# Layer 3 of a four-layer kernel: order of the sums on TensorE, and which engine multiplies states 3 and 12 by C

## The chip, the cores and the metric

The kernel runs on one core of a Trainium2 chip. The metric is device time in microseconds for one launch, the median of several runs. Engines: TensorE (PE, with its weight loads PEld), VectorE (DVE), ScalarE (ACT), GpSimd (POOL), and SyncE (SP), which here only issues DMAs.

## The reference

Four layers run one after another on an image batch of 8 x 64 channels x 64 x 64 in f32. The change touches layer 3 alone. That layer is a pair of bidirectional state-space scans (Mamba), first along t and then along f. Cut to what matters:

```python
xc = silu(causal_dwconv(xc, cw, cb))
dbl = xc @ xpw.T                       # dt (rank r), B and C (n = 16 states each)
dt = softplus(dbl[..., :r] @ dtw.T + dtb)
def step(h, inp):                      # for every channel d and state n
    dA = exp(dt_t[:, :, None] * A)
    h = h * dA + (dt_t * x_t)[:, :, None] * B_t[:, None, :]
    y = einsum('bdn,bn->bd', h, C_t)
```

So each of the 16 states needs: dA = exp(dt*A), the product du*B (du = dt*x), the recurrence h, the product h*C, and the sum of h*C over the states.

## The kernel before, in words

**Tiles.** In layer 3 one *step* handles 512 positions of 256 channels, laid out as a tile of 128 partitions x 1024 (two halves of channels side by side). There are 256 steps: 2 weight sets x 16 chunks x 4 groups x 2 directions (the list `steps` at the end of `layer3`). Each step runs over 16 states, so the loop `for i in range(total + 2)` in `stream` has 4096 iterations; `n` is the state, `i % 16`.

**Work for one state.** ScalarE makes dA (`decay`, L522), two iterations ahead or three. The product du*B comes from one of two places. For states 0, 3, 4, 7, 8, 11 to 15 GpSimd multiplies (`multiply_b`, L528), three iterations ahead. For states 1, 2, 5, 6, 9, 10 (`fed`, called `direct` in `stream`) TensorE makes it with eight 128x128 matmuls against a diagonal matrix (`expand`, L2257): into a PSUM tile of the `dA` ring for 1, 5, 9 (`lent`), into the single PSUM tile `mm` for 2, 6, 10. Both of a pair are issued in one iteration: 5 and 6 in iteration 3, 9 and 10 in iteration 7, 1 and 2 of the next step in iteration 15. VectorE scans (`scan`, L552). The product with C (`multiply_c`, L566) is GpSimd's for the states listed in `shared` and VectorE's for the others. TensorE then adds the product into the PSUM tile `acc` with four 64x512 identity matmuls (`gather` calling `quads`, L320); this is called the state's *sum* below. Groups named `acc<-h` are sums of GpSimd's states, those named `acc<-hc` of VectorE's.

**Buffers.** A state of GpSimd's is scanned into a tile `h` of a pool of three, is multiplied by C there in place, and holds the tile until its sum has been read. A state of VectorE's is scanned in place in its `dA` tile (a ring of two PSUM tiles), and its product goes to a tile `hc` (three). The products du*B and the exponents of the `fed` states share a pool `hb` of four, used in the order of the states. Rows of B and C, broadcast to 128 partitions, come by DMA into a pool `bc` of eight, fetched six states ahead (`fetch`, L2266 to L2270); a slot comes free when the C product of its state is done.

**What sets the order.** Nothing is reordered: every engine runs its instructions in the order in which the loop writes them. In an iteration that is: fetch, `multiply_b(i+3)`, GpSimd's `multiply_c(i-1)`, pieces of the next step's preparation (`plan` says how many and where), sums, other tasks (`advance`), `scan(i)`, further pieces, VectorE's `multiply_c(i)`, `decay` and `expand`. The pieces that matter here are the matmul to B, C and dt (L2195, written behind scan 2), the matmul for dt (L2207, iteration 3, before the scan), du on GpSimd (L2217, iteration 4), the gate's matmul (L2224, behind scan 6), the transposes of du (L2246, behind scan 10) and the convolution's matmul (L2180, behind scan 13). All of these use the single PSUM tile `mm`. State 0's sum is written behind scan 2 (`first`), with the skip term (`acc<-u,skip`) before it.

## Time and profile before

| what | value |
|---|---|
| median of 3 runs | 23591.48 us (23584.76 to 23625.18) |
| the profiled execution's own time | 23561.4 us |
| its span, first to last instruction | 23559.6 us |
| layer 3's scans, in the span | 11202 to 23551 us |
| VectorE busy in that stretch | 11846.8 of 12349.0 us |
| GpSimd busy in that stretch | 11478.2 us |
| TensorE busy (matmul / weight load) | 10683.0 / 5648.0 us |
| ScalarE busy | 9143.4 us |
| granted TensorE clock, DMA share | 0.95, 0.63 |

Costs of the operations that recur, mean of one:

| operation | engine, line | ns |
|---|---|---|
| product du*B | GpSimd, L528 | 2366 |
| product h*C | GpSimd, L566 | 2361 |
| product h*C | VectorE, L566 | 1225 |
| scan | VectorE, L552 | 2269 to 2282 |
| exponents, two of 512 columns | ScalarE, L522 | 689 to 711 each |

How to read it: a group's row in the profile names the line, engine, operation, what it writes and reads, and a count, then its busy time, the mean of one, and how long its engine was idle just before, with what ended most of that. Helpers hide the state number: all scans are L552 and all sums are L320, so a single state is found by its place in the timeline of a step. Between two scans the C product of VectorE makes the distance 3.45 us instead of 2.19. A step of 16 states takes 48.23 us on average, and the shortest about 46.5.

### The profile page before, as it was taken

To read this page: it belongs to the slowest core of one execution; us is meant where nothing else is said; L and a number is where in the kernel's file an instruction comes from. 1 tells how busy PE (TensorE), PEld (TensorE's weight loads), DVE (VectorE), ACT (ScalarE), POOL (GpSimd) and SP (SyncE) were. 2 spreads that over 40 slices of the span, in tenths; PEclk is the share of its full clock that TensorE was granted. 3 is DMA by queue.
4 is the path that set the end of the run, shared out by engine and by line. 5 is a ranking of instruction groups with operands and counts; after the bars stand their busy time and mean duration, and the time that the engine had idled before them with its cause. 6 is when DMAs were issued, how large, how long until landed. Compare 5 with 4: busy or idle time off the path is not lost. (4 is left out here: it accounts for less than half of the span.)

```text
span 23559.6 us, 306615 instructions
## 1 busy us (share of the span) xinstructions
PE 19078.5 (81%) x108058; PEld 8425.2 (36%) x108058; DVE 21365.9 (91%) x12265; ACT 14942.1 (63%) x19503; POOL 20571.2 (87%) x9876
## 2 busy tenths in 40 slices
PE   7757776777777788878888888888888888888888
PEld 5311221221221223322444444444444444444444
DVE  5599999999999769977999999999999999999999
ACT  5445555555555456632777777777777777777776
POOL 0499999999999749975999999999999999999999
PEclk9878888888888899989999999999999999999999
DMA  3599999899999759951666666666666666666665
GB/s 80 193 328 331 316 317 330 313 320 325 315 322 321 261 174 340 343 184 39 181 186 183 184 182 184 185 182 182 183 183 186 182 184 182 184 183 183 184 184 173
DMA packets 2857413, 5296.53 MB, mean 225 GB/s; under 512 B 1357208, under 2 KB 1363452, under 8 KB 2853568
## 3 DMA queue, kind: packets, MB, share of 16 engines
q1 hardware_dynamic: 2831296, 5213.58, 69.6%
q10 hardware_dynamic: 24576, 63.33, 0.7%
q8 instruction: 854, 13.99, 0.2%
q14 instruction: 687, 5.63, 0.1%
HBM read 5112.98 MB, written 162.40 MB: 224 GB/s over the span
## 5 line engine op out<-in xcount | busy, mean ns | idle before, releaser
L528 POOL TENSOR_TENSOR hb<-du,bc 128x1024 f32<-128x1024 f32 x3072 | 7222.4, 2364 | 619.2 <-DMA bc<-bc 253.6
L552 DVE TENSOR_TENSOR_SCAN dA<-dA,hb 128x1024 f32<-128x1024 f32 x2488 | 5675.5, 2281 | 187.3 <-POOL hb L528 113.4
L566 POOL TENSOR_TENSOR h<-h,bc 128x1024 f32<-128x1024 f32 x2208 | 5180.4, 2361 | 118.2 <-DVE h L552 109.9
L528 POOL TENSOR_TENSOR hb<-du,b 128x1024 f32<-128x1024 f32 x2048 | 4879.7, 2417 | 336.2 <-DVE h L552 121.2
L522 ACT ACTIVATE dA<-dt,w_A 128x512 f32<-128x512 f32 x5120 | 3520.3, 689 | 1508.2 <-DVE hc L566 716.3
L522 ACT ACTIVATE dA<-dt,w_l_A 128x1024 f32<-128x1024 f32 x2560 | 2857.6, 1117 | 997.6 <-DVE hc L566 756.7
L552 DVE TENSOR_TENSOR_SCAN dA<-dA,carry,hb 128x1024 f32<-128x1024 f32 x1320 | 3093.8, 2344 | 95.1 <-POOL hb L528 52.9
L566 DVE TENSOR_TENSOR hc<-dA,bc 128x1024 f32<-128x1024 f32 x2400 | 2939.1, 1225 | 141.4 <-issue 2.7
L320 PE MATMUL acc<-h,ident 64*64 64x512 f32 x16384 | 2165.9, 629 | 399.6 <-POOL h L566 397.4
L2257 PE MATMUL dA<-bc,duT 128*128 128x128 f32 x12288 | 1854.5, 313 | 616.0 <-ACT z L2233 596.1
L2257 PEld LDWEIGHTS dA<-bc,duT 128*128 128x128 f32 x12288 | 1700.7, 222 | 1225.0 <-ACT z L2233 800.8
L320 PE MATMUL acc<-hc,ident 64*64 64x512 f32 x16384 | 2085.5, 602 | 0.0
L522 ACT ACTIVATE hb<-dt,w_A 128x512 f32<-128x512 f32 x3072 | 2039.3, 711 | 10.7
L1290 PE MATMUL acc<-hc,ident 64*64 64x512 f32 x11264 | 1857.0, 756 | 142.6 <-DVE img L1410 84.1
L552 DVE TENSOR_TENSOR_SCAN h<-hb,mm 128x1024 f32<-128x1024 f32 x768 | 1742.4, 2269 | 236.0 <-PE acc L320 168.1
L1290 PE MATMUL acc<-h,ident 64*64 64x512 f32 x5120 | 976.6, 834 | 1130.8 <-POOL h L566 1122.0
L552 DVE TENSOR_TENSOR_SCAN h<-hb,dA 128x1024 f32<-128x1024 f32 x768 | 1752.6, 2282 | 129.0 <-PE dA L2257 83.7
L566 DVE TENSOR_TENSOR hc<-dA,c 128x1024 f32<-128x1024 f32 x1408 | 1723.7, 1224 | 116.0 <-DMA c<-bc 3.8
L552 DVE TENSOR_TENSOR_SCAN h<-dA,hb 128x1024 f32<-128x1024 f32 x712 | 1622.9, 2279 | 17.6 <-ACT dA L522 16.8
L2257 PE MATMUL mm<-bc,duT 128*128 128x128 f32 x12288 | 1571.3, 283 | 1.4 <-ACT u L2191 1.4
L566 POOL TENSOR_TENSOR h<-h,c 128x1024 f32<-128x1024 f32 x640 | 1520.9, 2376 | 19.5 <-ACT carry L1383 19.0
L2257 PEld LDWEIGHTS mm<-bc,duT 128*128 128x128 f32 x12288 | 1521.8, 202 | 2.2 <-ACT u L2191 2.2
(344 smaller groups left out, 26991.6 us busy)
## 6 DMA issues: line engine op xcount, KB each, us to landing
bc<-bc SPq DMA_DIRECT2D x2560, 512.0 KB
b<-bc SPq DMA_DIRECT2D x2048, 512.0 KB
c<-bc SPq DMA_DIRECT2D x2048, 512.0 KB
bc<-bc SPq DMA_DIRECT2D x512, 1024.0 KB
bc<-dg SPq DMA_DIRECT2D x1536, 256.0 KB
bc<-bc SPq DMA_DIRECT2D x1536, 256.0 KB
tmp<-rs SPq DMA_DIRECT2D x93, 512.0 KB
raw<-x SPq DMA_DIRECT2D x256, 128.0 KB
```

The source lines that it names most:

```text
L320: self.nc.tensor.matmul(acc[j * C : j * C + C, r * 512 : r * 512 + 512], lhsT(j)[at, at], rhs[at, j * 512 : j * 512 + 512], start=start, s ...
L522: nc.scalar.activation(o[:, cut], s.dt[:, cut], AF.Exp, scale=A[:, n : n + 1])
L528: nc.gpsimd.tensor_tensor(s.shaped(hb[i]), s.shaped(s.du), B.pop(i), ALU.mult)
L552: nc.vector.tensor_tensor_scan(h[:, way], dA[i][:, way], b[:, way], s.first(n), ALU.mult, ALU.add)
L566: engine.tensor_tensor(s.shaped(o), s.shaped(h), CC.pop(i), ALU.mult)
L1290: nc.tensor.matmul(o, lhsT[at, at], part, start=start, stop=stop)
L2257: nc.tensor.matmul(hb[:, at], self.duT[:, at], diag[:, m * 128 : m * 128 + 128], start=True, stop=True)
```

## The change

It does two things, both in layer 3. In iteration `i` the sum of state `i-2`, where that is one of GpSimd's, is now written behind VectorE's C product and ahead of `decay` and `expand`; it was written in the next iteration (as `gather(i - 3)`) before the scan. And the list `shared` loses 12 and gains 3.

```diff
                 work = None if work and work.over else work
-                if 2 < i <= total + 2 and shared(i - 3):
-                    gather(i - 3)
                 if 1 < i and not first and not shared(i - 2):
                     gather(i - 2)
...
                 if i < total and not shared(i):
                     multiply_c(i)
+                if 1 < i and shared(i - 2):
+                    gather(i - 2)
                 if not direct(i + 2):
                     decay(i + 2)
...
-                    self.shared = (1, 2, 5, 6, 9, 10, 12, 14)
+                    self.shared = (1, 2, 3, 5, 6, 9, 10, 14)
```

Built, the two kernels have the same instructions in the same numbers. ScalarE's and SyncE's order is the same. On TensorE the sums of states 1 and 5 now stand in front of the expansions of 5, 6 and of 9, 10, and those of 2 and 6 right behind them; state 12's sum, still in front of the expansions of 1 and 2, is no longer one that waits for GpSimd. On GpSimd, state 3's C product stands between the du*B product of state 7 and `du`, and state 12's is gone from between the du*B product of the next state 0 and the C product of 14. On VectorE scans 1 to 4 follow without state 3's C product between them, and state 12's stands between scans 12 and 13.

## The prediction

> **What bounds the kernel now.** I read the page first, then VectorE's waits inside layer 3, then the timeline of one step of layer 3. Busy tenths in 40 slices (page):

> ```profile
> DVE  5599999999999769977999999999999999999999
> POOL 0499999999999749975999999999999999999999
> PEclk9878888888888899989999999999999999999999
> ```

> Layer 3 is the second half: its scans run from 11202 to 23551 us, 256 steps of 16 states, 48.23 us a step. VectorE and GpSimd are both over 90% busy there. The part on the chain that ended last shows 0% everywhere (it breaks off near the end), so it is of no use, and I take VectorE's waits in that stretch (columns: total us, times, longest):

> ```profile
> DVE h L552 <- PE acc L320: 168.1, 213, 1.8
> DVE h L552 <- PE dA L2257: 83.7, 182, 1.9
> DVE h L552 <- ACT hb L522: 73.1, 49, 4.5
> DVE dA L552 <- POOL hb L528: 28.2, 5, 26.0
> DVE h L552 <- ACT dA L522: 27.0, 34, 0.8
> ```

> VectorE loses little: a step without any wait takes 46.49 us (the one that starts at 17040.5), so 1.74 us of 48.23 is waiting. All that this edit could ever win in layer 3 is 256 x 1.74 = 445 us (1.9%). "PE acc" is a scan that wants one of the three `h` buffers back, which the additions on TensorE (L320) still read. Now TensorE and VectorE in the step whose scan 2 ends at 17145.54 (start, us, engine, line, operation; idle before in brackets):

> ```profile
> 17145.60 1.93 PE L2195 MATMUL mm<-u,w_xp 128*68 128x512 f32 x4 [0.96 <-DVE h L552]
> 17147.46 1.09 PE L320 MATMUL acc<-u,skip 64*64 64x512 f32 x8
> 17148.37 1.04 PE L320 MATMUL acc<-hc,ident 64*64 64x512 f32 x8
> 17149.34 1.13 PE L2207 MATMUL mm<-dbl,both 4*128 4x512 f32 x4
> 17150.40 2.05 PE L2257 MATMUL dA<-bc,duT 128*128 128x128 f32 x16
> 17152.28 1.95 PE L2257 MATMUL mm<-bc,duT 128*128 128x128 f32 x16
> 17154.16 1.95 PE L320 MATMUL acc<-h,ident 64*64 64x512 f32 x16
> ...
> 17161.51 3.65 PE L2257 MATMUL dA<-bc,duT 128*128 128x128 f32 x16 [2.35 <-ACT z L2233]
> 17164.95 1.99 PE L2257 MATMUL mm<-bc,duT 128*128 128x128 f32 x16
> ```
> ```profile
> 17148.90 1.23 DVE L566 TENSOR_TENSOR hc<-dA,bc 128x1024 f32<-128x1024 f32 x1
> 17150.04 2.29 DVE L552 TENSOR_TENSOR_SCAN dA<-dA,hb 128x1024 f32<-128x1024 f32 x1
> 17152.36 1.22 DVE L566 TENSOR_TENSOR hc<-dA,bc 128x1024 f32<-128x1024 f32 x1
> 17153.50 2.28 DVE L552 TENSOR_TENSOR_SCAN h<-hb,dA 128x1024 f32<-128x1024 f32 x1
> 17155.69 2.26 DVE L552 TENSOR_TENSOR_SCAN h<-hb,mm 128x1024 f32<-128x1024 f32 x1
> ...
> 17165.26 2.29 DVE L552 TENSOR_TENSOR_SCAN h<-hb,dA 128x1024 f32<-128x1024 f32 x1 [0.34 <-PE dA L2257]
> ```

> To be seen: from scan 2's end TensorE works without a gap up to the du*B products of states 5 and 6 (17150.40 and 17152.28). State 5's product ends at 17152.45, only 1.05 us before scan 5 (17153.50), and what keeps scan 5 until then is state 3's and 4's C products on VectorE. Later TensorE idles 2.35 us, and state 9's product then takes 3.65 instead of 2.05.

> **The change, part by part.** Durations are of the one profiled execution (span 23559.6, time 23561.4 us; the median of the runs, 23591.48, lies 0.13% above). Means are over the 248 inner steps, from the timeline's rows. The frame is scan 2's end = 0.

> *State 3 to GpSimd, 12 to VectorE.* Counts stay: 8 products on each engine, 2361 ns on GpSimd (L566 POOL row), 1225 on VectorE. Scan 12 now runs in place like the others of VectorE's states (2281 against 2279 ns). On VectorE a C product between two scans adds 3.45 - 2.19 = 1.26-1.28 us, so state 3's leaves (-1.28), state 12's comes (+1.26): nothing by itself, but the scans 5 to 12 now want their inputs 1.28 us earlier.

> *Sum of state 1 ahead of state 5's product.* State 1's product on GpSimd ends at 0.32 (mean), so no wait is added, but TensorE reaches that point only at 4.9-5.1 in every step, and the sum takes its 0.91 us (start to start in the rows above) there. Expansion 5 ends now at 7.17 (mean; 6.91 in most steps), then at 7.17 + 0.91 = 8.08; a scan follows 0.10 later: 8.18. VectorE alone would be ready at 7.96 - 1.28 = 6.68. **New wait at scan 5: 1.50 us** (now 0.10). Queued behind on TensorE: expansion 6.

> *Scan 6's buffer.* The order of `h` buffers is now 1, 2, 3, 5, 6, ..., three deep, so scan 6 takes state 2's, and the sum of state 2 stands right behind expansion 6. Expansion 6 ends now at 8.96, then 9.87. Where a scan already waits for a sum behind an expansion, it starts 1.18 us after the expansion's end (0.91 plus release; state 10 in the median step): 11.05. VectorE: 8.18 + 2.19 = 10.37. **New wait 0.68** (now 0.12).

> *Scans 9 and 10.* Now they lose 0.94 us together: expansion 9 cannot start before state 7's C product frees its buffer (3.55 after scan 6's end), runs slow, and sum 5 stands behind expansion 10. After: GpSimd's order is product 7 (start 3.4, as scan 3 frees its buffer), **C 3**, du, B 8, C 5, five times 2.34: C 5 ends at 15.15, which is 2.1 after scan 6's new end (13.06-13.3; now 0.9 after). du waited 0.6 us for ScalarE before; that is absorbed. Sum 5 then ends 3.0 after scan 6's end, 0.5 ahead of the moment when expansion 9 may start. If TensorE stays warm, scans 9 and 10 go without a wait, as today in the steps where something else fills that gap (scan 10 at 9.08 after scan 6's end instead of 10.17). [...] I take 0.31: 0.1 each for the steps with an `xn` product in GpSimd's way (one in eight), for those where state 7's rows land late (44 of 248), and for a slow clock. Bounds 0.05 and 0.7.

> *Scans 1 and 2.* Now they lose 0.57: sum 12 waits for GpSimd's product 12 (0.3 after scan 15's end) and holds expansion 1. State 12 being VectorE's, that goes; expansion 1 then starts behind L2180 and sums 12 and 13, about 0.6-0.9 earlier. What is left is ScalarE's (the ACT hb row, in two steps of eight): 0.33. Bounds 0.2 and 0.57.

> *Other queues.* SP: state 11's rows go into state 3's buffer, now freed by GpSimd at 8.1 (16.7 after scan 0) and not by VectorE; SP issues them today at 17.0 on average, so nothing moves; if its slack were gone, B 11 has 2 us more. The next step's state 4 rows no longer wait for GpSimd's product 12 (issued 6 us earlier). GpSimd's B 8 ends at 12.8, scan 8 starts near 18.8; B 15 at 34, scan 15 at 37: covered. ScalarE's exponents keep their order and over 2 us.

> *Sum a step:* 1.50 + 0.68 + 0.31 + 0.33 = 2.82 of waiting against 1.74, so +1.08 us, x 256 = **+276 us** (1.2%): 23561.4 becomes 23837, the median 23591.5 becomes 23867. With the bounds, +0.68 to +1.75 a step: 23765 to 24040.

> **The rivals.**
> *Free additions, release early (faster).* The additions are small; if the array took sums 1 and 2 in the shadow of the du*B matmuls' weight loads, scan 5 would wait only 7.27 - 6.68 = 0.59 and scan 6 not at all: 0.59 + 0.31 + 0.33 - 1.74 = -0.51 a step, -130 us, 23461. It decides at 0.5 us: above it a sum ahead of expansion 5 eats what state 10 gains. Against: TensorE's rows are 0.91-0.97 from start to start around every such sum. 8%.
> *Free additions, release late (no change).* Scan 6 still 1.18 behind expansion 6: 0.59 + 0.68 + 0.31 + 0.33 - 1.74 = +0.17, +44 us, 23636: the wait has only moved from state 10 to 5 and 6. 9%.
> *GpSimd late and TensorE cold (slower still).* TensorE now stands waiting for C 5 with expansions 9 and 10 behind it. Spare is 0.5 us; if C 5 comes 0.5 later or the clock halves in three steps of four as now, sum 5 takes 1.9 and expansion 9 up to 3.65: 0.7 to 1.3 us more a step, 24050 to 24200. For it: GpSimd idles only 3.4 us a step. Against: the gap before it is shorter than today's. 17%.
> *As summed:* 66%.

> **How the numbers follow.** The prediction is the likeliest case, 23867. The range 23630 to 24120 takes in that case, the no-change case and the near half of the last; about 2 in 10 is left out. Faster or slower counts from 0.2% (47 us), about what a measurement of this kernel can tell: faster 0.08, same 0.09, slower 0.83.

> **What would show it.** VectorE's waits in layer 3: "h <- PE dA" grows from 84 to some 350 us, all at scan 5; "h <- PE acc" stays near 170 but sits at scan 6, not 10; state 9's expansions take near 2.05 on average; ACT hb stays near 70. Step length 49.3. I am wrong if scan 5 starts less than 7.5 us after scan 2's end (the sum costs nothing), or if waits for GpSimd's C 5 open in front of expansion 9.

## The result, and the profile after

The changed kernel takes 23929.75 us (median of 4 runs, 23922.62 to 23936.63) against 23594.22 us before (4 runs on the same chip): ratio 1.0142, 95% interval 1.0129 to 1.0155. That is 335.5 us, or 1.31 us for each of the 256 steps. The prediction was 23867 us, in the range 23630 to 24120.

The profiled execution took 23936.63 us with a span of 23934.8 us. The same three rows of the page as before:

```profile
DVE  5599999999999679977999999999999999999999
POOL 0499999999999669976999999989999999899998
PEclk9878887887888899999999999999999999999999
```

The rows hardly differ from those of before: a loss of 1.4% is invisible in tenths. The list of VectorE's waits in layer 3 (total us, times, longest) shows it:

```profile
DVE h L552 <- PE dA L2257: 402.3, 167, 3.6
DVE h L552 <- POOL h L566: 165.6, 127, 1.7
DVE h L552 <- PE acc L320: 137.7, 252, 0.6
...
DVE h L552 <- ACT hb L522: 14.6, 8, 4.0
```

"PE dA" grew from 83.7 to 402.3 us, and a wait for "POOL h" of 165.6 us appeared that did not exist. Where they sit is seen in the timelines of two neighbouring steps. First TensorE, then VectorE, in the step whose scan 2 ends at 16785.01 (the profile records each of these f32 matmuls twice, so x8 are the four of a sum):

```profile
16785.07 1.93 PE L2195 MATMUL mm<-u,w_xp 128*68 128x512 f32 x4 [1.26 <-DVE h L552]
16786.93 1.09 PE L320 MATMUL acc<-u,skip 64*64 64x512 f32 x8
...
16789.87 1.09 PE L320 MATMUL acc<-h,ident 64*64 64x512 f32 x8
16790.89 2.05 PE L2257 MATMUL dA<-bc,duT 128*128 128x128 f32 x16
16792.78 1.95 PE L2257 MATMUL mm<-bc,duT 128*128 128x128 f32 x16
```
```profile
16790.55 1.22 DVE L566 TENSOR_TENSOR hc<-dA,bc 128x1024 f32<-128x1024 f32 x1
16793.07 2.29 DVE L552 TENSOR_TENSOR_SCAN h<-hb,dA 128x1024 f32<-128x1024 f32 x1 [1.30 <-POOL h L566]
16795.91 2.29 DVE L552 TENSOR_TENSOR_SCAN h<-hb,mm 128x1024 f32<-128x1024 f32 x1 [0.55 <-PE acc L320]
```

The sum of state 1 (16789.87) now stands in front of expansion 5, which ends at 16792.94. Scan 5 follows 0.13 us later and has waited 1.30 us. The profile names GpSimd as its releaser only because GpSimd's product of state 3 happens to end at that moment (it started at 16790.71); scan 5 reads nothing of it. Then scan 6 waits 0.55 us for the sum of state 2.

The step before it (scan 2's end at 16734.83):

```profile
16734.88 2.74 PE L2195 MATMUL mm<-u,w_xp 128*68 128x512 f32 x4 [2.16 <-DVE h L552]
16737.55 1.93 PE L320 MATMUL acc<-u,skip 64*64 64x512 f32 x8
...
16741.32 1.09 PE L320 MATMUL acc<-h,ident 64*64 64x512 f32 x8
```
```profile
16744.53 2.29 DVE L552 TENSOR_TENSOR_SCAN h<-hb,dA 128x1024 f32<-128x1024 f32 x1 [2.94 <-PE dA L2257]
```

The order is the same, but TensorE had idled 2.16 us instead of 1.26, its first two entries take 2.74 and 1.93 us instead of 1.93 and 1.09, and all that follows is 1.64 us late: the clock granted to TensorE had fallen to half (0.50 from 16735.88 to 16739.29, shown in the last section). Scan 5 waits 2.94 us. These two kinds make up nearly all steps: of 256, 136 wait 1.2 to 1.8 us at scan 5, and 109 wait 2.8 to 3.2.

The ledger of VectorE's idle time just before a scan, averaged from the rows of the 248 inner steps, for all kernels of this study (the e runs are described below; us a step; "other" is every other scan):

| kernel | step | 1 and 2 | 5 | 6 | 9 and 10 | other |
|---|---|---|---|---|---|---|
| before | 48.20 | 0.41 | 0.08 | 0.10 | 0.80 | 0.01 |
| after | 49.63 | 0.08 | 2.05 | 0.55 | 0.14 | 0.00 |
| e1_order | 47.97 | 0.70 | 0.39 | 0.00 | 0.14 | 0.03 |
| e2_list | 51.69 | 0.00 | 3.36 | 0.00 | 1.45 | 0.00 |
| e3_late1 | 51.18 | 0.15 | 4.14 | 0.00 | 0.14 | 0.00 |
| e4_h4 | 50.41 | 0.31 | 1.81 | 0.00 | 1.37 | 0.13 |
| e4_bc7 | 50.79 | 0.28 | 1.97 | 0.55 | 1.05 | 0.06 |
| e5_warm | 49.14 | 0.05 | 1.53 | 0.55 | 0.18 | 0.00 |
| e6_swap11 | 47.65 | 0.38 | 0.34 | 0.00 | 0.05 | 0.16 |
| e7_swap11warm | 47.60 | 0.37 | 0.26 | 0.00 | 0.03 | 0.21 |
| e8_px12 | 48.34 | 1.09 | 0.42 | 0.00 | 0.11 | 0.02 |
| e8_px11 | 47.59 | 0.42 | 0.28 | 0.00 | 0.03 | 0.18 |
| e9_px11warm | 47.52 | 0.46 | 0.13 | 0.00 | 0.07 | 0.17 |
| e10_sum0late | 48.94 | 0.10 | 1.21 | 0.56 | 0.19 | 0.00 |

In every row the step less its waits is 46.7 to 46.9 us, so these waits are nearly the whole difference between the kernels. From before to after they grow from 1.40 to 2.82 us, times 256 is 364 us. The two profiled executions differ by 23936.63 - 23561.4 = 375.2 us (the one of before was lower than all its timed runs, so the medians differ by less).

### The profile page after: what moved, and what is told of

Read it like the earlier page. It is cut to its first block, busy times and chain, and to the rows that moved or that the text cites. A ratio compares the mean times of both kernels' runs of the same rounds, so it can differ in the third digit from the quotient of the medians.

```text
span 23934.8 us, 306585 instructions
## 1 busy us (share of the span) xinstructions
PE 19032.0 (80%) x108058; PEld 8082.7 (34%) x108058; DVE 21359.2 (89%) x12265; ACT 14930.6 (62%) x19503; POOL 20578.0 (86%) x9876
## 5 line engine op out<-in xcount | busy, mean ns | idle before, releaser
L528 POOL TENSOR_TENSOR hb<-du,bc 128x1024 f32<-128x1024 f32 x3072 | 7220.6, 2361 | 792.2 <-DVE h L552 347.6
L552 DVE TENSOR_TENSOR_SCAN dA<-dA,hb 128x1024 f32<-128x1024 f32 x2488 | 5677.0, 2282 | 190.8 <-POOL hb L528 109.6
L566 POOL TENSOR_TENSOR h<-h,bc 128x1024 f32<-128x1024 f32 x2208 | 5185.0, 2358 | 475.6 <-DVE h L552 444.7
L528 POOL TENSOR_TENSOR hb<-du,b 128x1024 f32<-128x1024 f32 x2048 | 4876.0, 2412 | 347.6 <-DVE h L552 126.1
L522 ACT ACTIVATE dA<-dt,w_A 128x512 f32<-128x512 f32 x5120 | 3524.5, 690 | 2095.7 <-DVE hc L566 1515.4
L522 ACT ACTIVATE dA<-dt,w_l_A 128x1024 f32<-128x1024 f32 x2560 | 2857.5, 1117 | 996.3 <-DVE hc L566 756.6
L552 DVE TENSOR_TENSOR_SCAN dA<-dA,carry,hb 128x1024 f32<-128x1024 f32 x1320 | 3093.3, 2343 | 93.8 <-POOL hb L528 55.2
L566 DVE TENSOR_TENSOR hc<-dA,bc 128x1024 f32<-128x1024 f32 x2400 | 2939.2, 1225 | 157.2 <-issue 3.1
L320 PE MATMUL acc<-h,ident 64*64 64x512 f32 x16384 | 2225.4, 631 | 520.6 <-POOL h L566 520.6
L552 DVE TENSOR_TENSOR_SCAN h<-hb,dA 128x1024 f32<-128x1024 f32 x768 | 1751.3, 2280 | 581.7 <-PE dA L2257 402.3
L320 PE MATMUL acc<-hc,ident 64*64 64x512 f32 x16384 | 2117.9, 611 | 0.0
L522 ACT ACTIVATE hb<-dt,w_A 128x512 f32<-128x512 f32 x3072 | 2039.4, 711 | 10.9 <-DVE h L552 0.2
L1290 PE MATMUL acc<-h,ident 64*64 64x512 f32 x5120 | 975.1, 833 | 1146.8 <-POOL h L566 1137.8
L552 DVE TENSOR_TENSOR_SCAN h<-hb,mm 128x1024 f32<-128x1024 f32 x768 | 1741.7, 2268 | 145.1 <-PE acc L320 137.7
L2257 PE MATMUL dA<-bc,duT 128*128 128x128 f32 x12288 | 1591.3, 284 | 317.9 <-issue 221.0
L566 DVE TENSOR_TENSOR hc<-dA,c 128x1024 f32<-128x1024 f32 x1408 | 1723.4, 1224 | 116.4 <-DMA c<-bc 4.2
L2257 PEld LDWEIGHTS dA<-bc,duT 128*128 128x128 f32 x12288 | 1455.9, 194 | 969.9 <-issue 483.1
L552 DVE TENSOR_TENSOR_SCAN h<-dA,hb 128x1024 f32<-128x1024 f32 x712 | 1622.8, 2279 | 16.4 <-ACT dA L522 16.3
L566 POOL TENSOR_TENSOR h<-h,c 128x1024 f32<-128x1024 f32 x640 | 1518.5, 2373 | 17.8 <-ACT carry L1383 16.6
L2257 PE MATMUL mm<-bc,duT 128*128 128x128 f32 x12288 | 1506.4, 276 | 1.4 <-ACT u L2191 1.4
```

The costliest lines, as they stand in the source:

```text
L320: self.nc.tensor.matmul(acc[j * C : j * C + C, r * 512 : r * 512 + 512], lhsT(j)[at, at], rhs[at, j * 512 : j * 512 + 512], start=start, s ...
L522: nc.scalar.activation(o[:, cut], s.dt[:, cut], AF.Exp, scale=A[:, n : n + 1])
L528: nc.gpsimd.tensor_tensor(s.shaped(hb[i]), s.shaped(s.du), B.pop(i), ALU.mult)
L552: nc.vector.tensor_tensor_scan(h[:, way], dA[i][:, way], b[:, way], s.first(n), ALU.mult, ALU.add)
L566: engine.tensor_tensor(s.shaped(o), s.shaped(h), CC.pop(i), ALU.mult)
L1290: nc.tensor.matmul(o, lhsT[at, at], part, start=start, stop=stop)
```

## The experiments

Medians, and ratios to the kernel before, which ran beside them on the same chip (its medians: 23580.01 us beside e1, e2, e3, e5; 23575.42 beside e4_h4, e8, e9; 23588.32 beside e4_bc7, e6, e7, e10):

| run | median us | ratio | 95% interval |
|---|---|---|---|
| e1_order | 23489.31 | 0.9965 | 0.9950 to 0.9979 |
| e2_list | 24440.0 | 1.0367 | 1.0351 to 1.0382 |
| e3_late1 | 24305.71 | 1.0312 | 1.0296 to 1.0327 |
| e5_warm | 23790.41 | 1.0091 | 1.0076 to 1.0106 |
| e10_sum0late | 23756.14 | 1.0069 | 1.0054 to 1.0084 |
| e4_h4 | 24128.7 | 1.0237 | 1.0221 to 1.0252 |
| e4_bc7 | 24209.2 | 1.0265 | 1.0250 to 1.0281 |
| e8_px12 | 23596.24 | 1.0007 | 0.9999 to 1.0016 |
| e8_px11 | 23410.17 | 0.9926 | 0.9909 to 0.9942 |
| e9_px11warm | 23384.43 | 0.9918 | 0.9903 to 0.9932 |
| e6_swap11 | 23427.55 | 0.9928 | 0.9913 to 0.9943 |
| e7_swap11warm | 23406.92 | 0.9921 | 0.9904 to 0.9937 |

Each edit is shown cut to what matters, against the changed kernel unless it says otherwise.

### e1_order: the new order alone

```diff
-                    self.shared = (1, 2, 3, 5, 6, 9, 10, 14)
+                    self.shared = (1, 2, 5, 6, 9, 10, 12, 14)
```

> The order of the sums alone; the list of GpSimd's states as before (3 VectorE's, 12 GpSimd's). Theory 1 (the loss is the chain on TensorE from scan 2's end to the sum of state 2, which only the list lays bare): faster than before by about 200 us, 23390, since scan 5 keeps state 3's C product ahead of it and scans 9 and 10 lose their 0.94 us a step. Rival (the sums ahead of the du*B matmuls are themselves what costs): slower than before by 200 us or more.

Measured: 91 us faster than before. The sign held, at under half the size. Its waits of VectorE in layer 3:

```profile
DVE h L552 <- PE dA L2257: 173.7, 112, 3.3
DVE h L552 <- ACT hb L522: 127.2, 76, 2.9
```

The 168 us of "PE acc" are gone, and scans 9 and 10 wait 0.14 us instead of 0.80. But 0.31 comes back at scan 5 and 0.29 at scans 1 and 2, where ScalarE's exponents and state 1's expansion are late. With the old list VectorE still multiplies state 3, so the sum in front of expansion 5 is mostly covered: scan 5 waits only in two kinds of step in eight.

### e2_list: the new list alone

```diff
+                if 2 < i <= total + 2 and shared(i - 3):
+                    gather(i - 3)
...
-                if 1 < i and shared(i - 2):
-                    gather(i - 2)
```

> The list alone (3 to GpSimd, 12 to VectorE); order of the sums as before. Theory 1: the slowest of all, some 430 us over before, near 24020: scan 5 waits 0.6 us, scan 6 waits 1.6 to 2 us for the sum of state 2, which now stands behind expansion 6 and the sum of state 1, and scan 10 keeps its 0.9. Rival (the order costs, the list is harmless): within 50 us of before.

Measured: 860 us slower than before, twice the expectation. VectorE's waits in layer 3, and one step whose scan 2 ends at 16940.98, TensorE and VectorE:

```profile
DVE h L552 <- PE acc L320: 993.0, 385, 7.3
```
```profile
16947.72 1.95 PE L2257 MATMUL mm<-bc,duT 128*128 128x128 f32 x16
16949.60 2.81 PE L320 MATMUL acc<-h,ident 64*64 64x512 f32 x24
```
```profile
16950.85 2.29 DVE L552 TENSOR_TENSOR_SCAN h<-hb,dA 128x1024 f32<-128x1024 f32 x1 [3.12 <-PE acc L320]
```

Scan 5 starts at 9.88, 1.18 us after expansion 6 has ended. That is the pattern of a scan that waits for a sum behind an expansion: with state 3 among GpSimd's, scan 5 takes the `h` buffer of state 1 (order 1, 2, 3, 5, three deep), and the sum of state 1 stands behind expansions 5 and 6. I had not seen that when I wrote the expectation.

### e3_late1: the changed kernel, with the sum of state 1 back behind expansions 5 and 6

```diff
-                if 1 < i and shared(i - 2):
+                if 1 < i and shared(i - 2) and n != 3:
                     gather(i - 2)
...
+                if n == 3 and 1 < i:
+                    gather(i - 2)
```

> The changed kernel with the sum of state 1 alone put behind the expansions of 5 and 6. Theory 1: within 50 us of the changed kernel (23930): scan 5's wait falls by 0.9 us a step, but scan 6 needs the sum of state 2, which is behind the same work in either order, so its wait grows by as much. Rival (it is the place of this one sum that costs): 0.91 us x 256 = 230 us come back, near 23700.

Measured: 24305.71 us, some 375 us over the changed kernel (390 when each is set against the kernel before that ran beside it), outside what either theory gave. The cause is the same oversight:

```profile
DVE h L552 <- PE acc L320: 1051.8, 253, 7.3
```

Scan 5 waits once in nearly every step for the sum of state 1, until 9.88 or 11.51 after scan 2's end, instead of 8.06 or 9.70. So the sum in front of expansion 5 is not an independent choice: once state 3 is GpSimd's, it is the cheaper of two bad places. e2 and e3 together show that the list makes the conflict, and the order softens it.

### e5_warm: the changed kernel, with work that keeps TensorE's clock up

Ahead of the sum of state 15, four matmuls add zero to the accumulator (a 128x128 tile of zeros as weights); the output is unchanged. They fill part of the gap that ends at L2195.

```diff
+                if n == 1 and i > NS:
+                    steps[at - 1].warm(acc[at - 1], hc[i - 2])
...
+            zero = cp.tile([128, 128], F32, name="zero")
+            nc.vector.memset(zero, 0.0)
...
+                def warm(self, acc, hc):
+                    net.quads(acc, lambda j: zero, hc)
```

> The changed kernel with four more 64x512 matmuls a step that add zero into acc, ahead of the sum of state 15, so that TensorE idles about 1.2 instead of 2.1 us before the matmul to B, C and dt. Theory 1 with the clock (the chain runs at half clock in three of eight steps because of that gap): expansion 5 ends 7.9 us after scan 2's end in nearly all steps, scan 5's wait falls from 2.1 to about 1.5 us, and the time by 100 to 160 us, near 23790, though there is more work. Rival (the clock has nothing to do with it): no change, or up to 100 us slower.

Measured: 23790.41 us, 140 us under the changed kernel (125 when each is set against the kernel before that ran beside it). VectorE's waits in layer 3:

```profile
DVE h L552 <- POOL h L566: 231.7, 178, 1.7
DVE h L552 <- PE dA L2261: 206.5, 118, 4.1
```

The two names together fall from 567.9 to 438.2 us, and the idle time before scan 5 from 2.05 to 1.53 us a step: 193 steps wait 1.2 to 1.8 us now, and 23 more than 2.8. By the granted clock 7 of the 256 starts of L2195 are slow, against 111 in the changed kernel. Nothing was taken off TensorE's queue, on the contrary; so it was the clock that made up the second part of scan 5's wait.

### e10_sum0late: the changed kernel, with the sum of state 0 moved behind the sum of state 2

This takes one sum out of TensorE's chain ahead of expansion 5 and leaves GpSimd's work as it is.

```diff
+                if begun[at] and plan:
+                    return
...
+                if n == 4:
+                    steps[at].add_up(acc[at], hc.pop(i - 4), False, False)
```

> The changed kernel with one thing less in the chain between scan 2 and scan 6: the sum of state 0 goes behind the sum of state 2. Nothing else moves. Theory 1 (scans 5 and 6 wait for the length of TensorE's chain: L2195, skip, sum 0, L2207, sum 1, expansions 5 and 6, sum 2): both start 0.91 us earlier, 233 us less than the changed kernel, near 23700. Rival (they wait for GpSimd's products 1 to 3, as the profile's releaser names at scan 5): no change from 23930.

Measured: 23756.14 us, 174 us under the changed kernel (168 when each is set against the kernel before that ran beside it). VectorE and GpSimd in the step whose scan 2 ends at 16695.40:

```profile
16702.60 2.29 DVE L552 TENSOR_TENSOR_SCAN h<-hb,dA 128x1024 f32<-128x1024 f32 x1 [0.45 <-PE dA L2261]
16705.44 2.29 DVE L552 TENSOR_TENSOR_SCAN h<-hb,mm 128x1024 f32<-128x1024 f32 x1 [0.55 <-PE acc L320]
```
```profile
16701.10 2.37 POOL L566 TENSOR_TENSOR h<-h,bc 128x1024 f32<-128x1024 f32 x1
```

Scan 5 starts at 7.20 instead of 8.06 and scan 6 at 10.04 instead of 10.90: each 0.86 earlier, about one sum's length on TensorE. Here scan 5 starts (16702.60) while GpSimd's product of state 3 still runs, until 16703.47. A scan that waited for that product could not have started, so this shows that the releaser "POOL h" in the profile was a coincidence, and that it is the length of TensorE's queue that sets scans 5 and 6. 190 steps wait under 1.2 us at scan 5. The rest of the expected gain is missing in 43 steps that wait 1.8 to 2.6 us, as 0.45 and the 1.64 of a slow clock would give, and in 23 that wait over 3.2 us. In these 23, of which 22 are the same one of every eight steps, the matmul for dt waits 1.6 to 1.9 us for ScalarE's copy of dbl, and TensorE works at half clock for 3.4 to 6.8 us between scan 2's end and scan 5's start:

```profile
13761.37 1.13 PE L2211 MATMUL mm<-dbl,both 4*128 4x512 f32 x4 [1.92 <-ACT dbl L2203]
```

### e4_h4 and e4_bc7: a fourth `h` buffer, and its control

A fourth buffer would free scan 6 of the sum of state 2. To make room for it the row buffers `bc` are cut from eight to seven, so the control has seven with three `h`.

```diff
-            pools = (pool("bc", 8), pool("hb", 4), pool("hc", 3), pool("h", 3), two(pool), pool("pa", 1, space=PSUM))
+            pools = (pool("bc", 7), pool("hb", 4), pool("hc", 3), pool("h", 4), two(pool), pool("pa", 1, space=PSUM))
```

> The changed kernel with four h buffers instead of three, paid for with seven instead of eight buffers for the rows of B and C. Theory 1: scan 6 then takes state 1's buffer, whose sum stands in front of expansion 5, so its 0.64 us of waiting a step goes: 165 us less than the changed kernel, near 23765, with scan 5's wait as it was. Rival (scan 6 really waits for expansion 6, and the buffer is only the last of two): no change. If the seventh row buffer matters, GpSimd's waits for DMA grow and eat part of it.

> The changed kernel with seven buffers for rows of B and C and three h buffers: what the fourth h buffer is to be compared with. Theory 1: slower than with four (24129) by about 165 us, near 24290, as scan 6 has its 0.64 us of waiting again. Rival (the fourth h buffer brought nothing, and its run is slow for another reason): within 40 us of 24129.

Measured: 24128.7 and 24209.2 us; both are slower than the changed kernel. The 0.55 us before scan 6 are gone in e4_h4 and there in the control, so that wait is the buffer, as predicted. But the gain of the fourth buffer is some 80 us (68 when each is set against the kernel before that ran beside it), half of what was expected or less: GpSimd's waits, of e4_h4 and then of e4_bc7, show what it does to take the eighth row buffer away:

```profile
POOL hb L528 <- DMA bc<-bc: 1009.2, 432, 13.6
```
```profile
POOL hb L528 <- DMA bc<-bc: 1013.7, 414, 13.9
```

GpSimd now loses 1000 us to late rows (176.3 us in the changed kernel), its product of state 5 comes late (it ends 3.28 and 2.44 us after scan 6's end on average, against 1.29), and scan 9 waits for expansion 9 behind sum 5 (scans 9 and 10: 1.37 and 1.05 us against 0.14). In e4_h4 VectorE arrives sooner at that wait, and gives back half of what it won. This pair also shows the rival "GpSimd late" in action: it is a real mechanism, which the changed kernel, with eight row buffers, does not run into.

### e8_px12, e8_px11, e9_px11warm, e6_swap11, e7_swap11warm: towards a faster kernel

e8_px12 is e1 with the sum of state 10 moved behind the convolution's matmul (L2180), to shorten the queue ahead of the expansions of the next states 1 and 2. e8_px11 has state 11 instead of 12 on GpSimd as well; e9 is e8_px11 with e5's zero matmuls. e6 is e1 with the list of e8_px11, without moving that sum; e7 is e6 with the zero matmuls. The first edit below is e8_px12's; the second is the list of e8_px11, e9, e6 and e7, against e1's.

```diff
+                if n == 13:
+                    gather(i - 3)
-                if 1 < i and shared(i - 2):
+                if 1 < i and shared(i - 2) and n != 12:
                     gather(i - 2)
...
-                    self.shared = (1, 2, 3, 5, 6, 9, 10, 14)
+                    self.shared = (1, 2, 5, 6, 9, 10, 12, 14)
```
```diff
-                    self.shared = (1, 2, 5, 6, 9, 10, 12, 14)
+                    self.shared = (1, 2, 5, 6, 9, 10, 11, 14)
```

> The order of the sums alone (list as before), and the sum of state 10 moved behind the convolution's matmul of the next step (L2180). In the run with the order alone, scans 1 and 2 lose 0.9 us a step because L2180 stands behind a sum that waits for GpSimd's product 10. Theory 1: these waits mostly go, 100 to 200 us less than the order alone, 23290 to 23390. Rival (ScalarE's own work makes scans 1 and 2 late): within 50 us of 23489.

> As the last one, but with state 11 instead of 12 on GpSimd, so that GpSimd's product is done before the sums ahead of expansions 1 and 2 are reached. Theory 1: scan 1 does not wait, 23250 to 23350. Against it: GpSimd's product 11 now stands ahead of the next state 0's du*B product, whose scan has some 0.9 us to spare; if that is used up VectorE waits for GpSimd at scan 0, and it is no faster than with 12.

> As the last one, with four matmuls a step that add zero into acc ahead of the sum of state 15. Theory 1: with expansions 1 and 2 early, TensorE idles over 2 us ahead of L2195 and runs the chain to expansion 5 at half clock in some steps; filled, scan 5 waits less, 30 to 120 us below the same kernel without them. Rival (state 3's C product on VectorE hides it): no change.

> The order of the sums alone, with state 11 instead of 12 on GpSimd. With the sum of state 10 also moved, this gave 23410 (23596 with 12). Theory 1: the move of sum 10 was no help in either, so this is 23300 to 23410; rival: it is what helped here, and this is 23450 or more.

> As the last one, with four matmuls a step that add zero into acc ahead of the sum of state 15, so that TensorE keeps its clock. 20 to 60 us less than without them, as in the pair with sum 10 moved (23410 and 23384).

e8_px12 missed: 23596.24 us, no different from before, where a gain over e1 was expected. VectorE's waits in layer 3:

```profile
DVE h L552 <- PE dA L2259: 341.9, 163, 4.4
DVE h L552 <- ACT hb L522: 47.1, 30, 3.6
```

"ACT hb" fell from 127.2 to 47.1 us as meant, but "PE dA" rose from 173.7 to 341.9, at scan 1: in two kinds of step in eight it waits 2.18 and 3.48 us for state 1's expansion, where e1 waits 0.72 and 1.94. The trace shows what stands ahead of that expansion in these steps, here in the one whose scan 1 starts at 16225.86, the sums of states 12 and 13:

```profile
16219.77 1.99 PE L320 MATMUL acc<-h,ident 64*64 64x512 f32 x8 [4.95 <-POOL h L566]
16221.53 1.93 PE L320 MATMUL acc<-hc,ident 64*64 64x512 f32 x8
```

The convolution's matmul now runs early, TensorE then idles (5.0 and 5.8 us in the medians of the two kinds) for GpSimd's product of state 12, and takes nearly twice as long for both sums (1.99 and 1.93 us in these rows, where a sum in the changed kernel's step above takes 1.09). So the gap was not removed but put right ahead of what scan 1 waits for. With state 11 in place of 12 the same order gives 23410.17 us, a gain, but short of the 23250 to 23350 expected. e6, without the move, is 23427.55 us, 17 us away with overlapping intervals, and between what its two theories gave: it is the list that helps, and not the moved sum. A reason that is in part argued: TensorE waits for GpSimd between the convolution's matmul and expansion 1 in 88 of e1's 246 inner steps and in none of e6's, and scans 1 and 2 lose 0.37 us instead of 0.70; and state 11 in GpSimd's list does not bring scan 5 forward by 1.28 us, as state 3 does. The zero matmuls bring 26 us (e9, where 30 to 120 was expected) and 21 us (e7), about as much as the runs scatter. e9_px11warm has the lowest median of the study, ratio 0.9918 (0.9903 to 0.9932); the intervals of e7 and e8_px11 overlap with its own.

## Why the prediction was right, point by point

The mechanisms of the likeliest case are the ones that the runs show, and the time lies 62.75 us above the forecast. The sum was 1.08 us a step, and the ledger says 1.42. Term by term (change in us a step; predicted as the new wait less the one it gave for now, measured from the ledger):

| term | predicted | measured |
|---|---|---|
| scan 5 | 1.50 - 0.10 = +1.40 | +1.97 |
| scan 6 | 0.68 - 0.12 = +0.56 | +0.45 |
| scans 9 and 10 | 0.31 - 0.94 = -0.63 | -0.66 |
| scans 1 and 2 | 0.33 - 0.57 = -0.24 | -0.33 |

That the waiting after the change was put at 2.82 us a step and is 2.82 in the ledger is luck: scan 5 waits 0.55 us more than forecast, and the other scans together 0.55 less. What makes the sum too low is the waiting before, put at 1.74 by comparison with the shortest step (46.49 us); the rows of the kernel before hold 1.40, since steps less their waits take 46.8 on average. (The upper bound of +1.75 adds up to +1.71 from the bounds of its terms; nothing hangs on it.)

*The sum of state 1 ahead of expansion 5* is where the size was off, by 0.57 us a step, and the clause that failed is "TensorE reaches that point only at 4.9-5.1 in every step". It did not hold of the kernel before either, where expansion 5 starts 4.85 us after scan 2's end in most steps, but later than 5.3 in 48 of 256. In the steps without a slow clock the mechanism is right: the sum starts at 4.86 and scan 5 at 8.06. That 8.18 was predicted for it is near by chance: the 7.17 that it is built on is a mean with the late steps in it, while 6.91 with the sum's 1.02 and 0.13 to the scan gives 8.06. In 109 steps, most of them with the sum at 6.49 and scan 5 at 9.70, the clock was slow.

The clock was slow because the gap ahead of L2195 had grown (median 2.16 us, before 0.96). These rows, of one step before and of one after, show by how much TensorE has come to run ahead: from L2180's start to L2195's it is 12.26 us, then 13.60.

```profile
16264.88 3.77 PE L2180 MATMUL mm<-xn,taps 128*128 128x512 f32 x8
16277.14 1.93 PE L2195 MATMUL mm<-u,w_xp 128*68 128x512 f32 x4 [0.96 <-DVE h L552]
```
```profile
16423.89 3.77 PE L2180 MATMUL mm<-xn,taps 128*128 128x512 f32 x8
16437.49 1.93 PE L2195 MATMUL mm<-u,w_xp 128*68 128x512 f32 x4 [2.16 <-DVE h L552]
```

The list does this, not the order: the median gap is 2.16 us in e2_list and 0.96 in e1_order. One would blame state 12's sum, which no longer waits for GpSimd. The rows speak against it: in the kernel before, TensorE waits for GpSimd between L2180 and expansion 1 in only 81 of 246 inner steps, and the gap ahead of L2195 is 2.23 us in these (median) and 0.96 in the others; and e6, where TensorE never waits there, has 0.96 as well. What fits these five kernels is the moved C product itself, though no run was made for it. From scan 10's end, behind which the transposes of du stand, to scan 15's end VectorE has one product more: 14.88 us (median) in the changed kernel and 14.87 in e2, 13.53 in the kernel before, e1 and e6. TensorE has the same work there, and so comes to the wait for scan 2 earlier by about that much. I had put the swap of states 3 and 12 down as "nothing by itself, but the scans 5 to 12 now want their inputs 1.28 us earlier", and did not ask what TensorE would do with the time behind these scans.

The slow clock accounts for 2.05 - 1.30 = 0.75 us a step, 192 us, in the rows, and e5 won 125 to 140 us of it back with zero matmuls that shorten the gap.

*Scan 6's buffer*: right. 0.55 us in nearly all steps, at 1.18 us after expansion 6, as predicted, named "PE acc" at 137.7 us (170 predicted), and gone with a fourth buffer.

*Scans 9 and 10*: right. Scan 10 starts 9.02 us after scan 6's end, as predicted (9.08) for steps in which something fills the gap; the row of the expansions into `dA` (states 1, 5 and 9) fell from 313 to 284 ns a matmul, and state 9's own expansion from 3.12 to 2.12 us on average (near 2.05 predicted). The gap ahead of that expansion fell with it, from 2.36 to 0.59 us (median), and the expansions that take over 2.5 us from 201 to 17 of 256. No run shows by itself the 0.1 us that the forecast's 0.31 holds for a slow clock; what the rows show is 0.14 for both scans, all causes together.

*Scans 1 and 2*: right in direction, and better than forecast; "ACT hb" fell to 14.6 us, where 70 was predicted. The cause that was given, sum 12's wait for GpSimd, can be only part of it: in e6 that wait is gone too, and scans 1 and 2 still lose 0.37 us. In most steps of the changed kernel expansion 1 starts 1.42 us after scan 15's end, in about half of e6's 2.58; so the head start told above is likely to have its part in it.

*The rivals.* "Free additions" falls: scan 5 starts at 8.06 and not before 7.5, the sum takes 1.02 us from start to start (16789.87 to 16790.89), and e10 gives 0.86 us back by moving another sum. "GpSimd late and TensorE cold" was half right in kind: the clock did fall, but at L2195 (111 of 256 starts) and hardly at expansion 9 (17 of 256 over 2.5 us), and not because GpSimd was late; e4 shows what that would have looked like. The test "PE dA near 350, all at scan 5" would have misled a reader who looked at the name alone: 402.3 us carry it, and 165.6 us of the same wait carry GpSimd's.

## What to carry to other kernels

In this kernel a sum in front of a product in TensorE's queue cost its full length once the consumer of that product was on time (in e10 one sum less brought scans 5 and 6 forward by 0.86 us each); so do not in the same change take away the work that kept the consumer busy until then (here state 3's C product on VectorE, 1.28 us). A list that says which engine does what also fixes the rotation of buffers, and the rotation decides which entry of a queue a scan must wait for: write out both before moving either (e2 is 860 us slower than the kernel before, e3 375 slower than the changed one). When work of one engine moves within a step, another engine can run ahead in the stretch that it was moved into: look at the gap that this opens (here on TensorE ahead of L2195, from 0.96 to 2.16 us in the median, with 111 of 256 starts behind it slow), and at what stands behind that gap.

## What the runs showed of the hardware

At L2195 TensorE's slow clock follows gaps of about 2 us. Sorted by the idle time ahead of L2195, with a slow start counted where L2195 and the skip term take over 3.3 us from start to the next sum (2.77 otherwise): in the changed kernel 0 of 58 starts are slow after less than 1.9 us, and 110 of 196 after 1.9 to 3; in the kernel before 0 of 193 and 24 of 60, and one after 4.4 us. The edge is sharp below 1.9 us; above it, the length of the gap alone does not decide. So a gap of 2 us there can be a cost: the zero matmuls of e5, which fill part of it, brought 125 to 140 us.

```profile
core 0: us, PE busy (x), PEclk, DMA share, GB/s
16732.47:16735.88 3.41, 1.25 (x7) 1.00 0.33 113
16735.88:16739.29 3.41, 3.41 (x11) 0.50 0.56 161
16930.44:16933.85 3.41, 1.50 (x4) 1.00 0.15 43
16933.85:16937.26 3.41, 3.41 (x26) 1.00 0.54 163
```

Both times TensorE idles 2.16 us ahead of L2195. The first gap (16732.72 to 16734.88, the step with the late scan 5 shown above) lies whole in one stretch of the grid, and the next stretch is granted half the clock. The second (16930.19 to 16932.35) is cut by an edge, 1.91 us of it lie in one stretch, and the clock stays full. Over the gaps ahead of L2195 in all 14 traces: of 666 with at least 2.03 us in one stretch every one is followed by half clock, of 2712 with less than 1.9 us none, and of the 206 between 53 (in the kernel before 25 of 25, none of 226 and 1 of 5; in the changed kernel 107 of 107, none of 124 and 4 of 25). So at this place it is the idle time within one stretch that decides, and kernels with the same median gap of 2.16 us differ in how their gaps fall on the grid: 38 of 256 starts are slow in e2_list, 111 in the changed kernel and 158 in e3_late1. How many of 256 will be slow could not have been read from the length of the gap.
